# A gated cross-attention and expert kernel: projections' copies moved between ScalarE's two exponentials, values copied for four batches at once, four tiles' statistics on VectorE, routing constants behind the spread keys

## The chip, the cores and the metric

The kernel runs on one core of a Trainium2 chip. A core has five engines that work side by side, each through its own queue in order: TensorE (PE; its weight loads are shown as PEld), VectorE (DVE), ScalarE (ACT), GpSimd (POOL) and SyncE (SP, which issues DMAs here). The metric is the device time of one execution in microseconds (us); lower is better.

## What is computed

All data is fp32. There are 16 batches of 128 rows with 128 columns, and a context of 77 rows with 96 columns for each batch.

```python
x = x + tanh(g_xattn) * xattn(layernorm(x), ctx)   # 16 heads of 8 columns
x = x + tanh(g_ffn) * experts(layernorm(x))

# xattn, for each batch
q = x @ Wq.T + bq;  k, v = split(y @ Wkv.T + bkv)
att = softmax(q @ k.T / sqrt(8));  out = (att @ v) @ Wo.T + bo

# experts: four rounds over the same four experts
for r in range(4):
    w = softmax(top2(cur @ Wg[r] + bg[r]))
    cur = cur + sum_e w[e] * (gelu(cur @ W1[e] + b1[e]) @ W2[e] + b2[e])
```

## The kernel before

The kernel has two stages. The first is a loop over the 16 batches (the attention loop, "turn" b for batch b). The second is the expert stage: the rows, in two halves of 1024, are sorted by their pair of experts through DRAM, and pieces of 128 rows go through the experts, eight phases of 21 pieces. The change edits only the first stage and what stands ahead of it.

The order of the work on PE, VectorE and ScalarE is the order in which the program is written; the GpSimd instructions made through `gp` (all of the compute instructions of the loop on POOL) are pinned in program order too. So the order of every queue is written out by hand: besides the fixed body of a turn there are lists of extra work for each turn, `early`, `extra`, `amid_exp`, `amid` and `behind` (L1054 on, filled up to L1195), each called at its place.

A turn b issues in this order (L1197 to L1242):

- POOL makes the spread keys of batch b+2 (`spread_keys`, tile `km`), unless they were made before;
- PE transposes the first half of the weights of batch b (`turn_weights`, tile `ps_tr`; ScalarE copies it into `exT`), `early[b]` follows, then PE computes the scores of batch b+1 (tile `sc`, two pairs of PSUM banks), then the other transposes of batch b;
- `extra[b]`: here lie the projections of the next group of four batches;
- `weights` of batch b+1 (L874): VectorE's maximum of the first half (`mx`), difference (`d`), ScalarE's first exponential (`ex`, 128x512), VectorE's second maximum, then `put_before` (L1211), then the second difference, ScalarE's second exponential and the exponential of the rest (128x208). `put_before` issues the output projection of batch b-1 (`put_out`: `ps_o` on PE, `rows` on VectorE) and the list `amid_exp[b]`. A ScalarE instruction issued there stands between the two exponentials in ScalarE's queue;
- `attend` of batch b (tile `ps_av`), `amid[b]`, then the reciprocal and product on VectorE (`over_sums`: `rs`, `oT`), and `behind[b]`.

The projections of a group i of four batches are: `turn_ctx` (transposed context, `ps_ct`, two copies into `ctxT`), `keys` (`ps_k`, copy into `kT`), `values_left` (`ps_vr`, copy into `left`, then POOL's product `vr`), `turn_x` (`ps_xt` into `xnT`), `queries` (`ps_q` into `qT`) and `values` (`ps_v`, copied by `values_done` into `vm`, for each batch two copies of 64x64). For groups 2 and 3 they lie in turns 4 to 7 and 8 to 11: context, then keys and the rest of the values, then queries, then values. The values of group 1 lie in turn 3. All of these PSUM tiles, `ps_av`, the transposed rows `ps_c` with their copies `gT`, the logits `ps_lg` (whose matmuls are in `amid[9]` and `behind[7]`), the counts `ps_n` (`behind[10]`) and the positions `ps_pos` (`behind[11]`) come from one pool of two banks, `p_m` (L103, `bank`), handed out in turn.

Layernorm statistics are of two kinds. `Norm` computes them on VectorE (`bn_stats`, `bn_aggr`, and one small addition in `scale`); `SumNorm` on ScalarE (L285 and L287, each with a sum read out). For both, `scale` ends with a power on POOL, for SumNorm after a small POOL instruction. `norms` are those of x ahead of the attention, `norms1` those of the rows behind it; one object can hold several tiles, and its scale is computed once, with the last tile's statistics.

`routing_constants` (L319) is a generator whose steps are called one by one; two of the steps hold eight POOL instructions each on the tile `keys` (not the attention's keys).

At the end of the loop the first half's rows are stored in sorted order by eight indirect DMAs from POOL (`scatter`, L556, tile `sorted`), each made to wait for a named piece of VectorE's work, and loaded again by SP (`load`). The expert stage begins with the transposes `ps_c` of those rows into `curT`.

Of the kernel before, what the change touches and what calls it, by code (L numbers as in the profile page):

```python
# [24 lines left out]
F32 = mybir.dt.float32  # L25
I32 = mybir.dt.int32
AF = mybir.ActivationFunctionType
# [6 lines left out]
DH = 8  # L34
# [12 lines left out]
def gated_xattn_moe(  # L47
# [20 lines left out]
    nc = tc.nc  # L68
    B, L, D = x.shape
    M, C = ctx_768.shape[1:]  # L70
    R, _, E = Wg.shape
    F = W1.shape[2]
    NF = F // P
    BB = 4
    NB = B // BB
# [19 lines left out]
    gp = Pinned()  # L95
# [27 lines left out]
    bqc = const.tile([P, 1], F32, name="bqc")  # L123
# [172 lines left out]
    def tp(*args):  # L296
        nc.tensor.transpose(*args)  # L297
# [100 lines left out]
    def advance(steps, n=None):  # L398

        while n is None or n > 0:  # L400
            try:
                next(steps)
            except StopIteration:
                return
            if n is not None:
                n -= 1
# [336 lines left out]

    def norm_of(table, kind, b, n):

        norm = kind(n, f"{n}{kind.__name__[0]}")
        for j in range(n):
            table[b + j] = norm, j

# [5 lines left out]
        norm, j = norms[b]  # L755
        norm.apply(j, row(b, 0, D), x_sb[:, b, :], eng)

    def turn_ctx(i):
        ps = bank("ps_ct")
        for j in range(BB):  # L760
            tp(ps[:C, ts(j, M)], ctx_sb[:, i * BB + j, :], ident[:M, :M])
        if i == 0:
            nc.scalar.copy(ctx0[0:C, :, :].rearrange("c b m -> c (b m)"), ps[:C, : BB * M])
        else:
            spread_ctx(
                ctxT[i % 2][0:C, :, :], ps[:C, : BB * M].rearrange("c (b m) -> c b m", m=M)
            )

    def spread_ctx(dst, src):
        for lo, n, m0, m1 in ((0, 2, 0, MP), (2 * MP, HR, MP, M)):  # L770
            nc.scalar.copy(
                dst[:, :, lo : lo + n * (m1 - m0)].rearrange("c b (n m) -> c b n m", n=n),
                src[:, :, m0:m1].unsqueeze(2).to_broadcast([src.shape[0], BB, n, m1 - m0]),
            )

    def keys(i):
        ps = bank("ps_k")
        mm(
            ps[:, : BB * M].rearrange("d (b m) -> d b m", m=M), wkT,
            ctxT[i % 2][:, :, MP : MP + M] if i else ctx0, start=True, stop=True,  # L780
        )
        nc.scalar.copy(kT[:, ts(i, BB), :].rearrange("d b m -> d (b m)"), ps[:, : BB * M])

    xnTs = {}

# [6 lines left out]
        xnTs[i] = awork.tile([P, TB], F32, tag="xnT", name="xnT")  # L792
        nc.scalar.copy(xnTs[i][:, at], ps[:, at])

    def queries(i, lo=0, hi=BB):
        ps = bank("ps_q")
        at = slice(lo * P, hi * P)
        mm(ps[:, at], wqT, xnTs.pop(i)[:, at], start=True, stop=True)
        nc.scalar.activation(qT[i][:, at], ps[:, at], AF.Identity, bias=bqc)

    pss_v = {}

    def values(i, done=True):
        ps = pss_v[i] = bank("ps_v")
        for j in range(BB):
            mm(ps[:, ts(j, D)], ctxT[i % 2][:, j, 0 : 2 * MP], wvT, start=True, stop=True)
        if done:
            for j in range(BB):
                values_done(i, j, nc.scalar.copy)

    def values_done(i, j, copy):
        for k in range(2):

            copy(
                vm[i % 2][ts(k, MP), j, :]
                .rearrange("m (j n) -> m j n", j=HP)[:, :, k * DH : k * DH + D]
                .rearrange("m j (g n) -> m j g n", g=NG)[:, :, :, 0:DH],
                pss_v[i][ts(k, MP), ts(j, D)]
                .rearrange("m (g j k d) -> m k j g d", g=NG, j=HP, k=2)[:, k],
            )  # L820

    def values_left(i):

        ps = bank("ps_vr")
        for j in range(BB):
            mm(
                ps[: HR * MR, ts(j, D)], ctxT[i % 2][:, j, 2 * MP : CT], wvT,
                start=True, stop=True,
            )
        v = ps[: HR * MR, :].rearrange("m (b d) -> m b d", d=D)  # L830
        if i == 0:
            return v
        left = awork.tile([HR * MR, BB, D], F32, tag="left", name="left", bufs=1)
        nc.scalar.copy(left, v)
        values_left_done(i, left, gp)

    def values_left_done(i, v, eng):
        eng.tensor_tensor(
            vr[i % 2], v, one_r.unsqueeze(1).to_broadcast([HR * MR, BB, D]), ALU.mult
        )  # L840
# [138 lines left out]
    turn_x(0, 1, 2)  # L979
    warm_tr(2)  # L980
    queries(0, 1, 2)
    values(0, False)
    left0 = values_left(0)
    warm_tr(3)
    ex = {0: weights(scs, lambda: values_done(0, 0, nc.scalar.copy))}
    values_left_done(0, left0, nc.vector)
    for j in range(1, BB):
        values_done(0, j, nc.vector.tensor_copy)
    for j in range(2, BB):
        norms0[2].apply(j - 2, row(j, 0, D), x_sb[:, j, :], gp)  # L990
    gp.memset(ctxT[1][C : C + 1, :, :], 1.0)
# [41 lines left out]
    def stats_x1(b):  # L1033
        norm, j = norms1[b]
        norm.stats(j, row(b, D, D))
        if j == norm.n - 1:
            norm.scale()
# [4 lines left out]


    for b, kind, n in (
        (0, SumNorm, 4), (4, Norm, 3), (7, Norm, 1), (8, SumNorm, 4), (12, SumNorm, 2), (14, Norm, 2)
    ):
        norm_of(norms1, kind, b, n)
    for b, kind, n in ((4, Norm, 2), (6, SumNorm, 2), (8, Norm, 4), (12, SumNorm, 4)):
        norm_of(norms, kind, b, n)
    by_sums = [b for b in range(B) if type(norms1[b][0]) is SumNorm]  # L1050

# [23 lines left out]
    behind[1] += [lambda: norms[6][0].scale(), lambda: norm_x(6, gp), lambda: norm_x(7, gp), lambda: gp.memset(vm[1], 0.0)]  # L1075
    extra[2] += [lambda: values_left(1), lambda: turn_x(1)]
    amid[2] += [lambda: queries(1)]
    extra[3] += [lambda: values(1)]
    behind[1] += [lambda: advance(constants, 1)]
    early[2] += [lambda: advance(constants, 2)]  # L1080
    for b in (2, 5, 6):
        behind[b] += [lambda: advance(constants, 1)]
    for b, j in ((1, 8), (2, 9), (2, 10), (3, 11)):
        behind[b] += [lambda j=j: stats_x(j)]
    for b, j in ((6, 12), (7, 13), (8, 14), (8, 15)):
        amid_exp[b] += [lambda j=j: stats_x(j)]
    for i in range(2, NB):
        b = (i - 1) * BB
        at = b + i - 2
        behind[at - 1] += [  # L1090
            lambda b=b: norms[b + BB][0].scale(), lambda b=b: norm_x(b + BB, gp),
            lambda b=b: norm_x(b + BB + 1, gp),
        ]
        early[at] += [lambda b=b: norm_x(b + BB + 2, gp), lambda b=b: norm_x(b + BB + 3, gp)]
        extra[b] += [lambda i=i: turn_ctx(i)]
        extra[b + 1] += [lambda i=i: keys(i), lambda i=i: values_left(i)]
        early[b + 2] += [lambda i=i: turn_x(i)]
        extra[b + 2] += [lambda i=i: queries(i)]
        extra[b + 3] += [lambda i=i: values(i)]
    for i in range(1, NB):  # L1100
        extra[i * BB - 1] += [lambda i=i: residual(i)]
    for b in by_sums:
        if b < 13:
            amid_exp[b + 2] += [lambda b=b: stats_x1(b)]
    for b, js in ((5, (0, 1)), (6, (2, 3)), (7, (4, 5, 6))):
        behind[b] += [lambda j=j: norm_x1(j, gp) for j in js]
    behind[8] += [lambda: norm_x1(7, nc.vector)]
# [89 lines left out]
    for b in range(B):  # L1197
# [13 lines left out]
        def put_before(b=b):  # L1211
            if b:
                put_out(b - 1, o.pop(b - 1), bank_tr)
            for f in amid_exp[b]:
                f()

        if b + 1 < B:
            ex[b + 1] = weights(scs, put_before)
# [305 lines left out]
```

## Time and profile before

| | us |
|---|---|
| median of 3 runs | 441.92 (441.75 to 443.85) |
| the profiled execution, its own time | 443.99 |
| its span, first to last instruction | 442.2 |
| first expert matmuls begin in it (`ps_h`) | 107.15 |
| mean granted TensorE clock | 0.989 |

By stretches of the span, busy us of each engine:

```profile
0.00:15.00 15.00, 13.89 (x102) 12.29 (x103) 11.46 (x34) 8.11 (x20) 8.63 (x24) 1.00 0.74 200
15.00:30.00 15.00, 14.59 (x212) 10.38 (x211) 14.30 (x34) 12.94 (x37) 11.11 (x36) 1.00 0.40 133
30.00:45.00 15.00, 12.65 (x178) 9.56 (x182) 12.19 (x23) 11.67 (x36) 12.36 (x29) 1.00 0.01 2
...
90.00:105.00 15.00, 10.88 (x180) 7.57 (x180) 13.82 (x32) 10.63 (x29) 10.25 (x13) 1.00 0.24 79
```

The columns are the stretch, its length, then PE, PEld, DVE, ACT and POOL busy with the number of instructions, the granted clock, the DMA share and GB/s. In the profile's lines "L905" is a line of the program, an operation is followed by output and input tiles with partitions x elements, "x8" is a count, and the bracket at the end says how long the engine stood idle before and what ended that. Lines of a timeline begin with start and duration; a merged line covers several instructions. Where one instruction overlaps the next on its engine, the step from start to start is shorter than the duration.

### The profile page before, as it was taken

The numbers are of one execution on the slowest core, as the hardware profiler recorded it, in microseconds if no ns is written. First come the engines' busy times: TensorE is split into PE (matmuls) and PEld (weight loads), VectorE is DVE, ScalarE is ACT, GpSimd is POOL, SyncE is SP. The second block draws the span as 40 slices with busy tenths as digits, with TensorE's granted clock in tenths as the row PEclk, the third lists the DMA queues.
The fourth block names the chain that finished last, engine by engine and source line by source line (L and its number), as shares of the span: only waits on it lengthen the run. The fifth ranks groups of instructions, "written<-read, shape, count | busy, mean of one in ns | idle before, by whom it ended". The sixth has DMA issues, their size and how long they took to land.

```text
span 442.2 us, 11648 instructions
## 1 busy us (share of the span) xinstructions
PE 418.7 (95%) x4170; PEld 391.4 (88%) x4170; DVE 341.8 (77%) x888; ACT 284.4 (64%) x936; POOL 223.5 (51%) x273
## 2 busy tenths in 40 slices
PE   9998999976999989999999999999999999999991
PEld 8775767655999989999999999999999999999991
DVE  7998897897667996987798599769867985874561
ACT  4878897856566656666566656656666665666661
POOL 7488857365036515841582475259326814650061
PEclk9999999998999999999999999999999999999996
DMA  6620000013012201400130131023011301310010
GB/s 163 192 99 1 1 1 2 21 70 110 1 50 64 87 1 63 136 1 27 63 112 3 49 102 49 2 74 123 1 37 66 99 0 63 130 50 8 0 34 16
DMA packets 19709, 24.03 MB, mean 54 GB/s; under 512 B 4099, under 2 KB 16708, under 8 KB 19524
## 3 DMA queue, kind: packets, MB, share of 16 engines
q1 hardware_dynamic: 15444, 13.43, 9.7%
q0 software_dynamic: 3584, 9.70, 6.2%
q8 instruction: 33, 0.54, 0.5%
q10 hardware_dynamic: 624, 0.17, 0.2%
q14 instruction: 24, 0.20, 0.1%
HBM read 13.58 MB, written 9.71 MB: 53 GB/s over the span
## 4 chain that ended last, share of the span: by engine, by line
PE 60%; issue 11%; POOL 9%; DVE 7%; DMA 5%; ACT 4%; SPq 1%; DVEq 1%; POOLq 0%; ACTq 0%
PE ps_y L294 26%; PE ps_h L294 26%; POOL out_dram L1287 4%; DMA wall<-in_L_ffn_W_dram 2%; PE ps_c L297 2%; POOL rows L93 2%; PE ps_tr L297 1%; DVE wb L1173 1%; PE ps_av L294 1%; DMA ctx_sb<-in_ctx_dram 1%; PE sc L294 1%; DVE rows L1273 1%; DMA sorted<-rows,pos_i 1%; DMA rows<-sorted 1%; PE ps_lg L294 1%
## 5 line engine op out<-in xcount | busy, mean ns | idle before, releaser
L1259 ACT ACTIVATE hT<-ps_h,wb 128x128 f32<-128x128 f32 x512 | 145.9, 368 | 83.4 <-ACT hT L1259 50.3
L294 PE MATMUL ps_h<-curT,wb 128*128 128x128 f32 x1024 | 136.5, 277 | 0.8 <-ACT curT L413 0.7
L294 PE MATMUL ps_y<-wb,hT 128*128 128x128 f32 x1024 | 135.7, 276 | 0.0
L294 PEld LDWEIGHTS ps_h<-curT,wb 128*128 128x128 f32 x1024 | 125.7, 193 | 1.2 <-ACT curT L413 0.9
L556 POOL DMA_INDIRECT sorted<-rows,pos_i x64 | 67.6, 1056 | 114.8 <-DVE start L549 49.4
L294 PEld LDWEIGHTS ps_y<-wb,hT 128*128 128x128 f32 x1024 | 124.5, 192 | 0.0
L1173 DVE COPY wb<-wall 128x1028 f32 x128 | 109.4, 856 | 12.2 <-issue 5.6
L93 POOL TENSOR_TENSOR lp<-rows,wg_rows 128x512 f32<-128x512 f32 x48 | 72.9, 1540 | 34.1 <-DVE rows L1273 31.2
L1273 DVE SCALAR_TENSOR_TENSOR rows<-ps_y,pws,rows 128x128 f32<-128x128 f32 x126 | 43.5, 346 | 35.9 <-PE ps_y L294 35.8
L1259 ACT ACTIVATE hT<-ps_h,wall 128x128 f32<-128x128 f32 x160 | 45.5, 369 | 32.7 <-PE ps_h L294 27.9
L294 PE MATMUL ps_y<-wall,hT 128*128 128x128 f32 x320 | 43.1, 278 | 0.0
L294 PE MATMUL ps_h<-cx,wall 128*128 128x128 f32 x320 | 42.3, 275 | 0.0
L294 PEld LDWEIGHTS ps_y<-wall,hT 128*128 128x128 f32 x320 | 38.9, 192 | 2.7 <-issue 1.7
L294 PEld LDWEIGHTS ps_h<-cx,wall 128*128 128x128 f32 x320 | 38.9, 192 | 0.0
L1287 POOL DMA_INDIRECT out_dram<-res,id_i x16 | 18.9, 1181 | 35.2 <-DVE res L1278 31.2
L453 DVE TENSOR_REDUCE lg<-lp 128x4 f32<-128x512 f32 x48 | 32.3, 673 | 3.1 <-POOL lp L93 3.1
L297 PEld LDWEIGHTS ps_tr<-ident,ex 128*128 128x128 f32 (+1 forms) x160 | 16.8, 139 | 17.7 <-ACT ex L892 9.4
L297 PE MATMUL ps_tr<-ident,ex 128*128 128x128 f32 (+1 forms) x160 | 26.2, 285 | 6.0 <-ACT ex L892 4.0
L883 DVE TENSOR_REDUCE mx<-sc 128x8 f32<-128x616 f32 x32 | 25.3, 791 | 3.9 <-PE sc L294 3.8
L886 DVE TENSOR_TENSOR d<-sc,mx 128x616 f32<-128x616 f32 x32 | 25.4, 794 | 1.7
L892 ACT ACTIVATE ex<-d 128x512 f32<-128x512 f32 x32 | 20.2, 633 | 6.7 <-DVE d L886 6.5
L1273 DVE SCALAR_TENSOR_TENSOR rows<-ps_y,pwxs,rows 128x128 f32 x40 | 14.0, 350 | 12.6 <-PE ps_y L294 9.9
(230 smaller groups left out, 495.6 us busy)
## 6 DMA issues: line engine op xcount, KB each, us to landing
rows<-sorted SPq DMA_DIRECT2D x16, 528.0 KB
wall<-in_L_ffn_W_dram SPq DMA_DIRECT2D x1, 1024.0 KB
wall<-in_L_ffn_W_dram SPq DMA_DIRECT2D x4, 256.0 KB
wg_rows<-wg_turned SPq DMA_DIRECT2D x1, 1024.0 KB
sorted<-rows,pos_i POOLq DMA_INDIRECT x64
x_sb<-in_x_dram SPq DMA_DIRECT2D x3, 256.0 KB
ctx_sb<-in_ctx_dram SPq DMA_DIRECT2D x4, 115.5 KB
out_dram<-res,id_i POOLq DMA_INDIRECT x16
```

Source lines behind the costliest of these rows:

```text
L93: return lambda *a, **kw: tc.keep_in_program_order(f(*a, **kw))
L294: nc.tensor.matmul(*args, **kw)
L297: nc.tensor.transpose(*args)
L453: nc.vector.tensor_reduce(lgs[h][:, t, :], prods.pop((h, t)), AX.X, ALU.add)
L556: ins = nc.gpsimd.indirect_dma_start(out=sorted_rows[h], out_offset=bass.IndirectOffsetOnAxis(ap=pos_i[:, t : t + 1], axis=0), in_=rows[h] ...
L883: beats.append(nc.vector.tensor_reduce(mx, sv, AX.X, ALU.max))
L886: nc.vector.tensor_tensor(d[:, ts(u, HR), :].rearrange("l (g h) m -> l g h m", h=HG), sv, mx.unsqueeze(3).to_broadcast([P, 2, HG, M]), ALU ...
L892: nc.scalar.activation(ex[:, ts(u, HR * MP)].rearrange("l (h m) -> l h m", m=MP), d[:, ts(u, HR), 0:MP], AF.Exp, scale=1.0 / math.sqrt(DH),)
L1173: nc.vector.tensor_copy(wb, wall[:, ds(e, 1), :].rearrange("p o n -> p (o n)"))
L1259: nc.scalar.activation(hT[:, fc, :], ps[:, ts(fc, P)], AF.Gelu_apprx_tanh, bias=wb[:, W_B + fc : W_B + fc + 1],)
L1273: return nc.vector.scalar_tensor_tensor(at, y, w, at, ALU.mult, ALU.add)
L1287: ins = nc.gpsimd.indirect_dma_start(out=out_rows, out_offset=bass.IndirectOffsetOnAxis(ap=id_i[:, t : t + 1], axis=0), in_=res, in_offset ...
```

## The change

It has five parts.

1. `values_done` copies four batches at once: four copies of 64x128 (64 partitions, 4 batches x 4 groups x 8 columns) in place of eight of 64x64. For group 0 all four are on VectorE, where before six were on VectorE and two on ScalarE.
2. `turn_ctx`, `keys`, `queries`, `values` and `values_left` take a `put`: with it, their copies out of PSUM are not issued at once but put on the list `copies`, which `put_before` issues ahead of `amid_exp[b]`. It is used for the values of group 1, and for all projections of groups 2 and 3 but the keys of group 3 (and `turn_x`).
3. Four tiles' statistics go from ScalarE to VectorE: of the rows behind the attention tiles 1 and 3, of x tiles 14 and 15. The objects are split: tiles 0 to 3 have one each (four scales in place of one), x's 12 to 15 two.
4. The places of the statistics that stay on ScalarE change: x's tile 13 goes from turn 7 to turn 8; of the rows, tile 9 from 11 to 12 and tile 10 from 12 to 13, where tile 11 is too.
5. One step of the routing constants (the second eight instructions on `keys`) goes from `behind[2]`, ahead of the spread keys of batch 5, to `early[3]`, behind them.

The diff, its core:

```diff
-        norm = kind(n, f"{n}{kind.__name__[0]}")
+        norm = kind(n, f"{len(table)}_{b}")
...
-        nc.scalar.copy(kT[:, ts(i, BB), :].rearrange("d b m -> d (b m)"), ps[:, : BB * M])
+
+        def done():
+            nc.scalar.copy(kT[:, ts(i, BB), :].rearrange("d b m -> d (b m)"), ps[:, : BB * M])
+
+        put(done) if put else done()
...
-        if done:
-            for j in range(BB):
-                values_done(i, j, nc.scalar.copy)
...
+        if put:
+            put(lambda: values_done(i, nc.scalar.copy))
+
+    def values_done(i, copy):
+        src = pss_v.pop(i).rearrange("m (b g j k d) -> m j k b g d", b=BB, g=NG, j=HP, k=2)
+        dst = vm[i % 2].rearrange("m b (j n) -> m j b n", j=HP)
+        for j in range(HP):
+            for k in range(2):
+
+                at = ts(k, MP)
+                copy(
+                    dst[at, j, :, k * DH : k * DH + D]
+                    .rearrange("m b (g n) -> m b g n", g=NG)[:, :, :, 0:DH],
+                    src[at, j, k],
+                )
...
-        (0, SumNorm, 4), (4, Norm, 3), (7, Norm, 1), (8, SumNorm, 4), (12, SumNorm, 2), (14, Norm, 2)
+        (0, SumNorm, 1), (1, Norm, 1), (2, SumNorm, 1), (3, Norm, 1), (4, Norm, 3), (7, Norm, 1),
+        (8, SumNorm, 4), (12, SumNorm, 2), (14, Norm, 2),
...
-    for b, kind, n in ((4, Norm, 2), (6, SumNorm, 2), (8, Norm, 4), (12, SumNorm, 4)):
+    for b, kind, n in (
+        (4, Norm, 2), (6, SumNorm, 2), (8, Norm, 4), (12, SumNorm, 2), (14, Norm, 2)
+    ):
...
-    extra[3] += [lambda: values(1)]
+    copies = []
+    put = copies.append
+    extra[3] += [lambda: values(1, put)]
...
-    for b in (2, 5, 6):
+    early[3] += [lambda: advance(constants, 1)]
+    for b in (5, 6):
         behind[b] += [lambda: advance(constants, 1)]
-    for b, j in ((1, 8), (2, 9), (2, 10), (3, 11)):
+    for b, j in ((1, 8), (2, 9), (2, 10), (3, 11), (6, 14), (7, 15)):
         behind[b] += [lambda j=j: stats_x(j)]
-    for b, j in ((6, 12), (7, 13), (8, 14), (8, 15)):
+    for b, j in ((6, 12), (8, 13)):
         amid_exp[b] += [lambda j=j: stats_x(j)]
...
-        extra[b] += [lambda i=i: turn_ctx(i)]
-        extra[b + 1] += [lambda i=i: keys(i), lambda i=i: values_left(i)]
+        extra[b] += [lambda i=i: turn_ctx(i, put)]
+        extra[b + 1] += [lambda i=i: keys(i, put if i < NB - 1 else None), lambda i=i: values_left(i, put)]
         early[b + 2] += [lambda i=i: turn_x(i)]
-        extra[b + 2] += [lambda i=i: queries(i)]
-        extra[b + 3] += [lambda i=i: values(i)]
+        extra[b + 2] += [lambda i=i: queries(i, put=put)]
+        extra[b + 3] += [lambda i=i: values(i, put)]
...
-    for b in by_sums:
-        if b < 13:
-            amid_exp[b + 2] += [lambda b=b: stats_x1(b)]
+    for b, at in ((0, 2), (2, 4), (8, 10), (9, 12), (10, 13), (11, 13), (12, 14)):
+        amid_exp[at] += [lambda b=b: stats_x1(b)]
...
-            for f in amid_exp[b]:
+            for f in copies + amid_exp[b]:
                 f()
+            copies.clear()
```

## The prediction

> **What bounds the kernel now.** I read the page's shares first, then the chain that ended last (to find which part of the span the change can move), then the timelines of GpSimd (POOL), ScalarE (ACT) and TensorE (PE) over the attention loop, since the change only edits that loop.
>
> ```profile
> span 442.2 us, 11648 instructions
> PE 418.7 (95%) x4170; PEld 391.4 (88%) x4170; DVE 341.8 (77%) x888; ACT 284.4 (64%) x936; POOL 223.5 (51%) x273
> ```
>
> PE is nearly full, but most of that is the expert stage after 107 us, whose instructions the change leaves as they are. The chain shows how the loop hands over to it:
>
> ```profile
> 96.87 1.07 POOL sorted L556
> ...
> 98.24 3.70 DMA sorted<-rows,pos_i
> ...
> 102.08 3.69 DMA rows<-sorted
> ...
> 105.82 0.67 PE ps_c L297 x4
> ```
>
> The eighth store of sorted rows, its landing, the reload, then the first expert piece. So the change is worth what it does to the moment of that store (98.24). It waits for VectorE's piece of work in turns 13 and 14 of the loop, hence for the pace of the whole loop. (Turn b: first transposes of batch b, scores of b+1, the other transposes, attend of b.) The turns last 4.5 to 7.8 us; at full pace PE needs 3.7 (transposes 0.5, scores 0.74, transposes 0.71, output 0.32, attend 1.45, starts to starts) plus the turn's projections. Three things hold it back. First, GpSimd's queue:
>
> ```profile
> 34.15 2.01 POOL L93 TENSOR_SCALAR keys<-num 128x8 f32<-128x8 f32 x8
> 36.23 0.70 POOL L93 TENSOR_TENSOR km<-kT,hmask 128x308 f32<-128x308 f32 x1
> 36.89 1.27 POOL L93 TENSOR_TENSOR x_sb<-x_sb,bo_b 128x512 f32<-128x512 f32 x1
> 38.12 1.04 POOL L93 TENSOR_TENSOR rstd4N<-rstd4N,half 128x4 f32<-128x4 f32 x1
> 39.27 1.58 POOL L93 TENSOR_SCALAR rows<-x_sb,mv4N,rstd4N 128x128 f32<-128x128 f32 x2
> 40.82 0.70 POOL L93 TENSOR_TENSOR km<-kT,hmask 128x308 f32<-128x308 f32 x1
> ```
>
> POOL is without a gap from 18.2 to 43.7 us, and PE's scores wait for its spread keys (km):
>
> ```profile
> 36.98 0.80 PE L294 MATMUL sc<-km,qT 32*128 32x308 f32 x8 [1.15 <-POOL km L93]
> 41.57 0.80 PE L294 MATMUL sc<-km,qT 32*128 32x308 f32 x8
> ```
>
> The second starts 0.05 us after its km ends (41.52). Second, VectorE: maxima, differences, rows, reciprocal and product of a turn are 4.5 us of starts to starts. Third, ACT's order: where projections' copies stand ahead of the first exponential, it starts late (34.49 after copies that ended at 34.46, its difference ready at 32.68).
>
> **The change, part by part.** All by this execution's timeline (span 442.2, own time 443.99).
>
> *The first group's values* (L814): VectorE's six copies (0.232 start to start, 1.39) and ACT's two become four on VectorE with twice the elements. No 64x128 copy in runs of eight is in the trace. Bounds: twice the price of a 64x64, 0.46 each (+0.46 us in all), or fixed cost plus 64 more elements at about 1 ns, 0.30 each (-0.19). I take -0.19: it is nearest to the 128x128 copy from PSUM (0.28 long). VectorE is full from 12 to 30 us, so this moves everything behind it.
>
> *Later groups' values*: ACT's eight copies (1.73) become four; the 128x128 copy takes 0.265, so 4 x 0.275 = 1.10, saving 0.63 in turns 3, 7 and 11.
>
> *Copies between the exponentials.* With sc the start of the scores, the rows give: first exponential possible at sc+2.56 (0.84 to the maximum, 0.90, difference 0.80), second at sc+4.25. So ACT has 1.7 us between them, 0.54 of it the first exponential. Values' 1.10 fit. Context's 1.03 with statistics' 0.82 do not (second exponential 0.7 late); queries' 0.58+0.82 miss by 0.25. In turn 3 the gain is plain: first exponential at 32.5 for 34.49, transposes no longer wait 0.86.
>
> *Constants behind the spread keys; norms split in single tiles.* Ahead of km for turn 4 go 8 key steps (-2.08), but tile 0's scale comes in (0.28+0.55) and tile 1's power (0.55, as rstd1N's 0.57): km ends at 36.93-2.08+1.38 = 36.23, less 0.19: the scores at 36.1 for 36.98. For the next km nothing has left: the eight key steps are now just behind the first km, and still ahead of this one, with the bias and four norms. POOL has no gap in which to hide the 1.38, so km ends at 41.52+1.38-0.19 = 42.7 and the scores start at 42.76 for 41.57: **+1.19**. PE would be ready at 40.7. Tiles 2 and 3 add 1.38 again before the next km, which ends near 46.3; PE asks for it only near 48.8, so that costs nothing (cover: POOL's old idle 1.79 at 43.74 and PE's delay).
>
> *A copy held back holds its PSUM bank.* Projections, attend, logits, counts and positions rotate through two banks, so each matmul group waits for the copy of the group two before it. The Trainium skill (PSUM — Partial Sum Buffer, Summary: rules for kernel authors) says "Evacuate promptly", which speaks against this change altogether. The row is narrower: in turn 9
>
> ```profile
> 68.01 0.58 ACT L834 COPY left<-ps_vr 104x512 f32<-104x512 f32 x1 [0.51 <-PE ps_vr L294]
> 68.49 0.59 ACT L413 COPY gT<-ps_c 128x512 f32<-128x512 f32 x1
> 68.97 1.38 ACT L892 ACTIVATE ex<-d 128x512 f32<-128x512 f32 x2
> 70.26 0.37 ACT L896 ACTIVATE ex<-d 128x208 f32<-128x208 f32 x1
> ```
>
> ```profile
> 68.65 0.65 PE L294 MATMUL ps_av<-exT,one 128*32 128x128 f32 x16
> ```
>
> attend starts when "left" ends (68.59). By the rule all ten groups moved cost; by the row only those whose bank PE wants again before the first exponential is over. By the rule, the ten at the 0.5 to 1 us of a first exponential and a copy would be 5 to 10 us; by the row I count four places:
> - turn 5: attend needs keys' copy, which now follows the first exponential (45.3+0.54+0.38): 46.29 where PE is ready at 45.92. Shift of the next turn **+1.35**.
> - turn 7: logits wait for values' copy, as before (57.77, logits 57.83). ACT does it 0.63 faster and without waiting ahead of the exponential, but VectorE now has tile 14's statistics (0.42) behind the two constants (0.80): its idle 0.43 before the maximum at 54.34 is gone, maximum at 55.73, exponential 57.45, copies to 59.09: shift **+1.31**. The 1.7 us that ACT won go to VectorE.
> - turn 9: gT's copy stays ahead of the exponential, "left" goes behind it: ps_c ends 69.2, gT 69.27, exponential 69.75, left 70.29 to 70.87, attend 70.92 for 68.65: shift **+2.27**. This is the largest.
> - turn 10: counts need the bank of queries' copy (77.52+0.54+0.69): 78.8 for 76.15. Turn 11: positions need values' copy (82.99+0.54+1.10): 84.7 for 81.67. Shift **+3.0** for PE, +2.65 for VectorE's maximum in turn 12.
>
> *Statistics.* Four tiles leave ACT (4 x 0.82) and cost VectorE 0.42 to 0.60 each. Tile 1 (turn 2) lies in the 0.55 that VectorE waited at 30.97, tile 3 (turn 4) in its wait for the late scores of turn 5, tile 15 (turn 7) just fits, tile 14 is counted. Two tiles now stand in turn 13 (10 and 11): 1.64 between the exponentials. Tile 11's sums end 98.6 by the shifted clock; POOL's scale of 8 to 11 and the seventh and eighth store are queued behind them: **+0.3**.
>
> *Sum at the eighth store*: +3.0 + 0.3 = +3.3. VectorE has a wait of 1.23 us in turn 13 (88.84, for PE) that no row explains; without it in both kernels the same walk gives +2.9, VectorE's maximum in turn 14 being then due 2.6 later and the store 0.3 more. I take **+3.1**. The profiled execution took 443.99, 2.07 above the median of 441.92 (443.85 also occurred); the difference is put on the median: 441.92 + 3.1 = **445.0 us**.
>
> **The rivals.**
> 1. *The freed exponential decides; faster.* PE's waits for the exponential are 4.0 us in four places; 0.86 (35.18) and 0.73 (65.36) are of the kind the change removes, and the wait for km of 1.15 goes too: -2.7, so 439.2. For it: these are the waits that the trace names. It needs POOL to give back the 1.38 before km of turn 5 (if that km ended by 40.7) and attend of turn 9 not to be held. Against it: POOL's gapless row, and the bank order. Chance 0.13.
> 2. *Only POOL's part lasts.* +1.2, the bank waits covered by slack elsewhere (PE loses 1.16 in turn 13 and 1.47 in turn 14 waiting for others): 443.1. Within what a measurement can tell from no change, which I set at 0.5% (2.2 us). Chance 0.20.
> 3. *More than counted*: the four-batch copies cost twice a 64x64, so nothing is saved (+0.65 at VectorE's start, +0.6 in turns 7 and 11), or turn 13's unexplained wait grows: 447. Chance 0.11. This is also the case in which "four at once" does not do what it says.
> The likeliest keeps 0.56, from 443.6 to 446.6.
>
> **How the numbers follow.** Slower by over 0.5% (above 444.1): nearly all of the likeliest (0.54) and case 3: 0.65. Within: case 2 and an edge: 0.22. Faster: 0.13. The range from 442.0 to 447.5 leaves out rival 1 and the far end of case 3.
>
> **What would show it.** Right: in the profile after, POOL gapless up to km of turn 5, which ends near 42.7, and the scores of that turn waiting for it about 2 us; attend of turn 9 starting as "left" ends, near 71; the first exponential of turn 3 near 32.5; the eighth store 3 us later; the expert stage's length unchanged. Wrong: the scores of turn 5 before 42, POOL with gaps before, or attend of turn 9 starting as the transposes' copies allow.

## The result and the profile after

| | before | after |
|---|---|---|
| median of 20 runs each, us | 442.16 (440.04 to 445.46) | 445.87 (441.85 to 448.3) |
| the profiled execution, its own time, us | 443.99 | 445.78 |
| its span, us | 442.2 | 444.0 |
| first expert matmuls (`ps_h`) begin, us | 107.15 | 109.25 |
| from there to the end of the span, us | 335.05 | 334.75 |

The ratio of after to before is 1.0061, 95% interval 1.0039 to 1.0084: about 2.7 us slower (0.0061 x 442), inside the predicted range. It is not the quotient of the medians (1.0084): the runs lie in groups, and a median can jump from one group to the next. In the two profiles all of the difference arises in the attention loop. Two things are easily misread here. The two profiled executions differ by only 1.8 us, less than the medians (3.7), because the profile of before has 1.9 us in turn 13 that after's has not (7.04 us from scores to scores, where the same turn takes 5.11 and 5.12 in experiments 10 and 11). And the profile of after runs 0.36 us late from the start (VectorE's first values' copies begin at 12.76 for 12.40).

The page of after begins with the same picture as before: PE full, ScalarE's 30 instructions fewer and VectorE's nine more.

```profile
span 444.0 us, 11631 instructions
PE 418.9 (94%) x4170; PEld 392.4 (88%) x4170; DVE 343.4 (77%) x897; ACT 278.8 (63%) x906; POOL 229.3 (52%) x278
```

Next comes what PE waited for in the loop, 29 to 100 us. Each row names the matmul and its line, the releaser, the microseconds in all, how often, and the longest. First before:

```profile
PE ps_tr L297 <- ACT ex L892: 3.1, 3, 1.5
PE ps_tr L297 <- ACT exT L905: 1.4, 2, 1.2
PE sc L294 <- POOL km L93: 1.1, 1, 1.1
PE ps_c L297 <- POOL rows L93: 0.4, 1, 0.4
...
```

The same view of after:

```profile
PE sc L294 <- POOL km L93: 3.6, 2, 2.2
PE ps_tr L297 <- ACT ex L906: 1.8, 3, 1.1
PE ps_o L294 <- ACT exT L919: 1.2, 5, 0.5
PE ps_lg L294 <- ACT vm L826: 0.7, 1, 0.7
PE ps_pos L294 <- ACT vm L826: 0.6, 1, 0.6
PE ps_av L294 <- ACT gT L413: 0.5, 1, 0.5
PE ps_n L294 <- ACT qT L806: 0.4, 1, 0.4
...
```

The change did what it says on ScalarE: the waits for the exponential fall from 3.1 to 1.8 us. The waits for the spread keys rise from 1.1 to 3.6, and four waits for copies out of the two banks, which the list of before doesn't have, appear: three for copies that the change holds back (0.7, 0.6 and 0.4) and one for `gT` (0.5), whose bank attend takes in turn 9. GpSimd's timeline of after shows where the first comes from:

```profile
34.37 0.19 POOL L93 TENSOR_SCALAR rstd<-mv 128x1 f32<-128x1 f32 x1
34.65 1.10 POOL L93 TENSOR_TENSOR rstd<-rstd,half 128x1 f32<-128x1 f32 x2
35.72 0.70 POOL L93 TENSOR_TENSOR km<-kT,hmask 128x308 f32<-128x308 f32 x1
36.50 2.01 POOL L93 TENSOR_SCALAR keys<-num 128x8 f32<-128x8 f32 x8
38.57 1.28 POOL L93 TENSOR_TENSOR x_sb<-x_sb,bo_b 128x512 f32<-128x512 f32 x1
39.81 1.03 POOL L93 TENSOR_TENSOR rstd<-rstd,half 128x4 f32<-128x4 f32 x1
40.95 1.59 POOL L93 TENSOR_SCALAR rows<-x_sb,mv,rstd 128x128 f32<-128x128 f32 x2
42.50 0.70 POOL L93 TENSOR_TENSOR km<-kT,hmask 128x308 f32<-128x308 f32 x1
```

The eight key steps now stand behind the first `km` (35.72) and ahead of the second (42.50); two scales (1.35 us, 34.37 to 35.72) have come in ahead of the first. No row has an idle bracket. PE's timeline shows who pays, in turns 4 and 5 and then in turn 9:

```profile
36.47 0.80 PE L294 MATMUL sc<-km,qT 32*128 32x308 f32 x8 [1.41 <-POOL km L93]
...
43.26 0.91 PE L294 MATMUL sc<-km,qT 32*128 32x308 f32 x8 [2.19 <-POOL km L93]
44.10 1.54 PE L297 MATMUL ps_tr<-ident,ex 128*128 128x128 f32 x6
...
48.03 0.64 PE L294 MATMUL ps_av<-exT,one 128*32 128x128 f32 x16
...
71.30 0.64 PE L294 MATMUL ps_av<-exT,one 128*32 128x128 f32 x16 [0.45 <-ACT gT L413]
```

The scores of turn 5 wait 2.19 us and start at 43.26 for 41.57. The row to be surprised at is the next: six transposes take 1.54 us, where six take 0.87 and 0.88 at this place in experiments 6 and 9. By stretches of 3.41 us, with the granted clock in the third column from the end:

```profile
40.45:43.86 3.41, 1.22 (x16) 0.69 (x12) 1.92 (x6) 2.29 (x8) 3.30 (x5) 0.99 0.02 5
43.86:47.27 3.41, 3.41 (x16) 2.78 (x13) 2.30 (x3) 1.81 (x4) 2.83 (x6) 0.50 0.00 0
47.27:50.68 3.41, 3.41 (x68) 2.92 (x70) 2.40 (x6) 1.96 (x5) 1.99 (x17) 1.00 0.00 0
```

In the stretch that holds the wait PE was busy for 1.22 us of 3.41; in the next the granted clock is 0.50, then 1.00 again. In the profile of before the only such stretch is at 107.6, behind the wait for the reload of the sorted rows.

The end of the loop, from the chain of after in order of time: the reload and the first expert pieces, 2.1 us later than before. The eighth store starts on POOL at 100.33 for 98.24.

```profile
104.06 3.82 DMA rows<-sorted
...
107.92 0.67 PE ps_c L297 x4
```

### The profile page after: what moved, and what is told of

Read it like the earlier page. It is cut to its first block, busy times and chain, and to the rows that moved or that the text cites. A ratio compares the mean times of both kernels' runs of the same rounds, so it can differ in the third digit from the quotient of the medians.

```text
span 444.0 us, 11631 instructions
## 1 busy us (share of the span) xinstructions
PE 418.9 (94%) x4170; PEld 392.4 (88%) x4170; DVE 343.4 (77%) x897; ACT 278.8 (63%) x906; POOL 229.3 (52%) x278
## 4 chain that ended last, share of the span: by engine, by line
PE 63%; DVE 11%; issue 11%; POOL 9%; ACT 3%; DMA 1%; DVEq 0%; POOLq 0%
PE ps_y L294 26%; PE ps_h L294 26%; POOL out_dram L1308 4%; DVE d L900 3%; DVE mx L897 2%; PE ps_c L297 2%; POOL rows L93 1%; PE ps_tr L297 1%; PE ps_warm L294 1%; PE sc L294 1%; DVE wb L1193 1%; PE ps_bh L294 1%; DMA rows<-sorted 1%; ACT ex L906 1%; PE ps_lg L294 1%
## 5 line engine op out<-in xcount | busy, mean ns | idle before, releaser
L556 POOL DMA_INDIRECT sorted<-rows,pos_i x64 | 71.4, 1116 | 108.4 <-DVE start L549 57.6
L919 ACT COPY exT<-ps_tr 128x512 f32<-128x512 f32 x32 | 18.5, 578 | 11.8 <-PE ps_tr L297 11.5
```

The source lines that it names most:

```text
L556: ins = nc.gpsimd.indirect_dma_start(out=sorted_rows[h], out_offset=bass.IndirectOffsetOnAxis(ap=pos_i[:, t : t + 1], axis=0), in_=rows[h] ...
```

## The experiments

Theory A, from the prediction with one addition: GpSimd's order puts 1.4 us ahead of the spread keys of turn 5, the wait lets the clock fall to half, and that is most of the loss. Theory B: the copies held behind the exponential keep their banks, and that is most of it. Theory C: it is VectorE's additional statistics. Each batch of four kernels shared its runs of the kernel before. In the first batch (experiments 1 to 4) these had a median of 443.91, against 442.16 to 442.89 elsewhere, so ratios are best compared within a batch. The kernel after did not run in the first batch: the ratios of 1 to 3 can't be put against its 1.0061, and what they show is read from their traces.

**1. Scales of the rows' tiles 0 to 3 later.** After, with these four scales in turn 5.

```diff
-        if j == norm.n - 1:
+        if j == norm.n - 1 and b > 3:
             norm.scale()
...
+    early[5] += [lambda k=k: norms1[k][0].scale() for k in range(4)]
```

> The changed kernel with the four scales of the rows' tiles 0 to 3 issued in turn 5, behind the spread keys that PE waits for, so that nothing of the split norms stands ahead of them on GpSimd. GpSimd theory: the spread keys for turn 5 end 1.4 us earlier (41.8 on the changed kernel's clock), PE waits 0.8 us for them in place of 2.19, TensorE's clock stays full behind that wait, and the expert stage begins 2 to 2.6 us earlier; time about 443.5. Bank theory (copies held back cost most): turn 5 starts earlier but at most 1 us of it lasts; time 445.

Measured: 444.59, ratio 0.9998 (0.9968 to 1.0027). Scores of turn 4 start at 35.10, those of turn 5 at 41.89, still behind a wait of 2.20, because PE came there earlier. Attend follows them by 3.56 us: no half clock there, although the wait is as long as in after. PE was busy for more of the stretch of 3.41 us in which it waited, 1.81 us in place of 1.22:

```profile
40.29:43.70 3.41, 1.81 (x16) 1.32 (x17) 2.08 (x6) 2.02 (x6) 3.41 (x6) 1.00 0.00 0
```

The norms' 1.35 us are a real part of the lateness: set to zero at turn 3, as in the table below, the scores of turn 12 come 1.40 later than in before, where they come 2.85 later in after. Taken away alone, they leave the wait.

**2. The second eight constants later as well.** Experiment 1 plus:

```diff
-    early[3] += [lambda: advance(constants, 1)]
+    early[5] += [lambda: advance(constants, 1)]
```

> The same, and the second eight routing constants are issued in turn 5 too. GpSimd theory: the spread keys of turns 4 and 5 no longer hold PE at all, scores of turn 5 start near 41 in place of 43.26, no low clock behind them, the expert stage begins about 3.3 us earlier than in the changed kernel; time 442.4, that of the kernel before or a little less. Bank theory: not over 1 us better than the changed kernel, 445.

Measured: 444.73, ratio 1.0014 (0.999 to 1.0038). The scores of turn 5 start at 40.43 with a wait of 0.40, but in turn 7 the transposes of the first norm rows wait for GpSimd:

```profile
52.95 0.33 PE L297 MATMUL ps_c<-ident,rows 128*128 128x128 f32 x1 [1.02 <-POOL rows L93]
53.72 0.33 PE L297 MATMUL ps_c<-ident,rows 128*128 128x128 f32 x1 [0.45 <-POOL rows L93]
```

The clock is at half behind that, from 55.0 to 58.4. So it is not the place of one step that binds. GpSimd has too much to do before turn 7; moved inside that stretch, work only moves the wait (the shift at turn 12 is 1.57).

**3. Three kinds of copies at once again.** After, with keys, left rows and queries copied where before copied them (context and values still held).

```diff
-        extra[b + 1] += [lambda i=i: keys(i, put if i < NB - 1 else None), lambda i=i: values_left(i, put)]
+        extra[b + 1] += [lambda i=i: keys(i), lambda i=i: values_left(i)]
-        extra[b + 2] += [lambda i=i: queries(i, put=put)]
+        extra[b + 2] += [lambda i=i: queries(i)]
```

> The changed kernel with the copies of keys, of the rest of the values and of queries issued at once again; those of context and values stay between the exponentials. GpSimd theory: scores of turn 5 unchanged at 43.2, PE's waits in turns 9 and 10 (0.45 and 0.41) go, time 445.2. Bank theory: 1.5 us or more come back, time 444 or less.

Measured: 444.98, ratio 1.000 (0.9971 to 1.0029). The waits of turns 9 and 10 (0.45 and 0.41) are gone, that of turn 11 is 0.85 for 0.60; the 2.21 us of turn 5 and the half clock behind it (44.9 to 48.3) stay. This ratio taken alone favours B, but after was not in the batch. The trace doesn't favour it: set to zero at turn 3, the scores of turn 12 come 2.75 later than in before, against 2.85 in after, so only 0.1 us of the loop's lateness goes with the three kinds of held copies. Experiment 12 repeats the question on another base.

**4. Constants alone.** Before, with the second eight constants behind the spread keys of turn 4, as the change has them.

```diff
-    for b in (2, 5, 6):
+    early[3] += [lambda: advance(constants, 1)]
+    for b in (5, 6):
         behind[b] += [lambda: advance(constants, 1)]
```

> The kernel before with one part of the change alone: the second eight routing constants behind the spread keys of batch 5. GpSimd theory: the wait of 1.15 us for the spread keys in turn 4 goes, but the spread keys for turn 5 stand behind the same work as before, scores of turn 5 start at 41.57 still, and the time stays at that of the kernel before (0.3 us either way). Rival, that the named wait is the price: 1.1 us faster.

Measured: 443.88, ratio 0.9989 (0.9968 to 1.0009). PE's timeline:

```profile
36.10 0.80 PE L294 MATMUL sc<-km,qT 32*128 32x308 f32 x8
41.95 0.80 PE L294 MATMUL sc<-km,qT 32*128 32x308 f32 x8 [1.12 <-POOL km L93]
```

The wait of 1.15 in turn 4 has become one of 1.12 in turn 5, and nothing is won.

**5. The kernel after once more**, in the second batch (experiments 5 to 8).

> The changed kernel itself, as the measure for the others on the same chip. Every theory: 1.006 of the kernel before, about 2.7 us more. Clock theory: its time falls into steps of about 1.8 us, as the half-clock stretches behind PE's waits are one or two.

Measured: 444.8, ratio 1.0054 (1.0013 to 1.0095). The wait in turn 5 is 2.22, the half clock runs from 43.6 to 47.0, attend follows the scores by 4.78. So this is no accident of one execution.

**6. PE kept busy in the wait, too long.** After, with matmuls of zeros ahead of the scores of turns 4 and 5.

```diff
+        if b in (4, 5):
+            warm_tr({4: 10, 5: 18}[b])
         if b + 1 < B:
             scs = scores(b + 1, kms.pop(b + 1))
```

> The changed kernel with 10 and 18 idle matmuls on zeros ahead of the scores of turns 4 and 5, where PE waits for the spread keys; nothing else. Clock theory: the scores of turn 5 still start when the spread keys end (about 43.2), but the granted clock stays at 1.00 behind them in place of 0.50 for 3.4 us, attend of that turn starts 3.5 us behind the scores in place of 4.8, and the time falls by 1.2 us. Queue theory alone (the clock costs nothing of its own): attend follows the scores as late as before, time the same.

Measured: 445.21, ratio 1.0059 (1.0037 to 1.0082). A miss of my own: each matmul of zeros appears as two in the profile, and the 36 of turn 5 took 4.18 us and ended 2.4 us behind the keys (scores at 45.68). Attend followed by 3.56, but the lateness ate that. Experiment 9 repeats it with the right count.

**7. Single scales alone.** Before, with the norm of tiles 0 to 3 split in four (statistics left on ScalarE).

```diff
-        (0, SumNorm, 4), (4, Norm, 3), (7, Norm, 1), (8, SumNorm, 4), (12, SumNorm, 2), (14, Norm, 2)
+        (0, SumNorm, 1), (1, SumNorm, 1), (2, SumNorm, 1), (3, SumNorm, 1), (4, Norm, 3), (7, Norm, 1), (8, SumNorm, 4), (12, SumNorm, 2), (14, Norm, 2)
```

> The kernel before with one part alone: the rows' tiles 0 to 3 get a scale each, all on ScalarE's sums as before. It adds 0.83 us on GpSimd for each tile, two of them ahead of the spread keys for turn 5, and removes the common scale of 1.23 later. GpSimd theory: scores of turn 5 start 1.7 us later than in the kernel before (43.2), PE waits some 1.6 us for them; time 1 to 2.5 us more, the most with a half-clock stretch behind the wait. Bank theory: no loss over 0.5 us, as no copy is moved.

Measured: 443.43, ratio 1.0026 (1.0009 to 1.0044). Scores of turn 4 at 37.77 behind a wait of 2.07, the clock at half from 39.2 to 42.6, scores of turn 5 at 43.57 for 41.57. The wait stands one turn earlier, since the constants are still in front; the price is of the kind that A names. The shift at turn 12 is 1.43.

**8. Scales and constants out of the way.** After, with the four scales in turn 5 (experiment 1) and the constants behind the norm rows that turn 7 needs.

```diff
-    early[3] += [lambda: advance(constants, 1)]
-    for b in (5, 6):
-        behind[b] += [lambda: advance(constants, 1)]
+    early[7] += [lambda: advance(constants, 2)]
+    amid[9] += [lambda: advance(constants, 1)]
```

> The changed kernel with GpSimd's queue put in order: the four scales in turn 5, the last two GpSimd steps of the routing constants in turn 7 where GpSimd waits over 4 us, their VectorE step in turn 9 where VectorE waits 1.9 us for logits. GpSimd theory: no wait of PE for spread keys or rows in turns 4, 5 and 7, 3 us less than the changed kernel, so at the kernel before or up to 1 us under it. Bank theory: 1 us less than the changed kernel.

Measured: 442.26, ratio 0.9984 (0.996 to 1.0009); the runs lie between 438.49 and 443.7, and the profile is of one of the three fastest (438.6). Scores of turn 5 at 39.31, first expert matmuls at 102.97. With GpSimd relieved, the loss of the change is gone, and a gain over before is not shown.

**9. PE kept busy in the wait, the right length.** As 6, with `{4: 6, 5: 7}`.

> The kernel after with 12 matmuls of zeros ahead of the scores of turn 4 and 14 ahead of those of turn 5, sized from the run with 20 and 36 (0.116 us each), so that they end when the spread keys do (36.3 and 43.2) and not 2.4 us behind. Clock theory: TensorE is not idle in the 2.2 us wait, the granted clock stays 1.00 from 43 to 48, the output's matmuls (attend) follow the scores of turn 5 by 3.5 us and not 4.8, later turns are 1.2 us earlier, ratio to the kernel before 1.003. Rival: a 3.4 us stretch at half clock is only moved to the next place with waits (the run with too many zeros had one at 64 us), and the ratio stays at 1.005 to 1.006.

Measured: 445.24, ratio 1.006 (1.004 to 1.0079). PE's timeline in turn 5:

```profile
40.59 1.73 PE L294 MATMUL ps_warm<-zero 128*128 128x128 f32 x14
42.95 0.80 PE L294 MATMUL sc<-km,qT 32*128 32x308 f32 x8 [0.64 <-POOL km L93]
43.69 0.88 PE L297 MATMUL ps_tr<-ident,ex 128*128 128x128 f32 x6
...
46.52 0.64 PE L294 MATMUL ps_av<-exT,one 128*32 128x128 f32 x16 [0.34 <-ACT kT L785]
```

The stretches of the same kernel:

```profile
39.75:43.16 3.41, 2.77 (x38) 2.39 (x34) 2.32 (x6) 2.67 (x9) 3.30 (x5) 1.00 0.02 5
43.16:46.58 3.42, 3.08 (x30) 2.31 (x30) 2.60 (x5) 1.91 (x5) 3.23 (x6) 1.00 0.00 0
```

The scores can start no earlier than in after (42.95, with 0.31 of it the earlier start of this execution), but PE is busy 2.77 us of the stretch in place of 1.22: the next one is at full clock, the six transposes take 0.88 for 1.54, attend follows the scores by 3.57 for 4.77. The half clock is therefore a consequence of PE's idleness, and costs 1.20 us here. The loop in this execution is earlier by that still in turn 14 (scores at 94.81 for 96.35, 0.34 of it from its earlier start). The median isn't: in this profile another half stretch has come up in the expert stage, at 162 to 165.4, behind a wait of 1.61 for VectorE that before and after have too, without the clock falling there. So the theory's expectation held for the place, and the rival's for the time. Only one execution of each kernel has a trace, but the mean granted clock of every run is on record: over the 20 runs of this kernel it averages 0.988, over the 20 of after 0.983. There was less half clock on the whole (the mean takes in the idle end of the kernel too), and the ratio is the same. So the 1.20 us are shown for this place in the trace; that they are a part of the loss in the time is not shown.

**10. GpSimd's part alone.** Before, with experiments 4 and 7 together: constants behind the keys of turn 4 and four single scales; copies, statistics and banks as before.

> The kernel before with GpSimd's part of the change alone: second constants behind the spread keys of turn 4, four single scales for tiles 0 to 3; copies, statistics and banks as before. If GpSimd's order makes the first half of the loss: scores of turn 5 start near 42.7 for 41.57 after a wait of about 2 us, the waits of turns 9 to 11 for copies are absent, and the ratio is 1.003 (1.1 us) to 1.005 (with a stretch at half clock behind the wait). If the held copies make all of the loss: 1.000. If GpSimd makes all of it: 1.006.

Measured: 445.25, ratio 1.0063 (1.004 to 1.0085), as much as the whole loss. (All four tiles stay on ScalarE's sums here, so 0.28 us more than in the change stand ahead of the keys of turn 5.) PE's timeline, then the stretches:

```profile
36.55 0.80 PE L294 MATMUL sc<-km,qT 32*128 32x308 f32 x8
...
44.23 0.96 PE L294 MATMUL sc<-km,qT 32*128 32x308 f32 x8 [2.93 <-POOL km L93]
```

```profile
41.32:44.74 3.42, 0.52 (x8) 0.31 (x8) 0.62 (x2) 1.35 (x4) 3.31 (x5) 1.00 0.02 5
44.74:48.15 3.41, 3.41 (x20) 2.63 (x13) 2.31 (x3) 1.28 (x3) 2.38 (x5) 0.50 0.00 0
```

All of the wait stands in turn 5: in turn 4 the keys are in time, since PE comes there later (its transposes wait 0.86 for the exponential, as before). The half clock follows. The two parts don't add up: alone they shift turn 12 by -0.13 (experiment 4) and +1.43 (experiment 7), together by +2.82, since only together do they stand ahead of the same keys. Of the four outcomes expected, "GpSimd makes all of it: 1.006" came in.

**11. Before, with only its constants moved**, as in 8: two steps to turn 7, one to turn 9.

```diff
-    for b in (2, 5, 6):
-        behind[b] += [lambda: advance(constants, 1)]
+    early[7] += [lambda: advance(constants, 2)]
+    amid[9] += [lambda: advance(constants, 1)]
```

> The kernel before with only its constants moved: GpSimd's two steps from turns 2 and 5 to the front of turn 7, VectorE's step from turn 6 to turn 9. If GpSimd's load ahead of the spread keys is what holds the first turns: scores of turn 4 near 35.8 (36.98 before), of turn 5 near 40.4 (41.57 before), and the ratio is 0.995 to 0.998. If the gain of the kernel after with the same move comes from the change's copies instead, this one stays at 1.000.

Measured: 440.36, ratio 0.9943 (0.9922 to 0.9963): faster than before and after. What PE waits for in its loop, 29 to 100 us:

```profile
PE ps_tr L297 <- ACT ex L892: 3.1, 4, 1.0
PE ps_o L294 <- ACT exT L905: 0.6, 3, 0.2
PE ps_tr L297 <- ACT exT L905: 0.5, 2, 0.2
...
```

No wait for `km` and none for `rows` is left. The waits for the exponential, which the change set out to remove, are all still there, and it is the fastest kernel of the study.

**12. Experiment 8 with keys, left rows and queries copied at once** (the diff of 3 on top).

> The kernel after with scales and constants moved (0.9984), and keys, left rows and queries copied at once again, as in the kernel before. If the held banks cost: the waits for the copies of gT (0.45) in turn 9 and of queries (0.41) in turn 10 are gone, the loop is 0.5 to 1 us shorter, ratio 0.996. If the exponentials of those turns become late by the same amount, or the waits are slack: 0.998 as without it.

Measured: 441.5, ratio 0.9968 (0.9949 to 0.9987). The waits for gT and queries are gone, the one in turn 11 is 0.85 again; set to zero at turn 3, the scores of turns 10 and 12 start 0.6 and 0.4 us earlier than in 8 (68.94 and 80.51 for 69.54 and 80.87). The step in the ratio is of that size (0.0016, 0.7 us), but the intervals overlap: holding these three kinds of copies costs a few tenths of a microsecond or nothing, and no gain from it is seen. Against 11 (same batch) this kernel is 1.1 us behind in the median, so the rest of the change doesn't pay either where GpSimd is relieved; in the traces 0.65 of it stand in turn 13, which takes 5.77 us with two tiles' sums between the exponentials and 5.12 in 11.

**The loop, turn by turn.** Start of the scores against before, in us, each kernel set to zero at the scores of turn 3:

| turn | before, start | after | GpSimd's part alone (10) | constants moved (11) |
|---|---|---|---|---|
| 4 | 36.98 | -0.67 | -1.21 | -1.22 |
| 5 | 41.57 | +1.53 | +1.88 | -1.14 |
| 6 | 47.41 | +2.94 | +3.29 | -1.03 |
| 7 | 53.51 | +1.93 | +2.80 | -2.03 |
| 8 | 59.30 | +2.54 | +2.82 | -2.02 |
| 10 | 72.08 | +2.48 | +2.81 | -1.96 |
| 12 | 83.04 | +2.85 | +2.82 | -1.95 |
| 13 | 87.63 | +2.78 | +2.82 | -1.95 |
| 14 | 94.67 | +1.52 | +0.89 | -3.87 |

GpSimd's part alone makes its shift in turns 5 and 6, gives 0.5 of it back in turn 7 and then keeps the rest. The kernel after makes much the same shift in turns 5 and 6, wins 1.0 by turn 7 (0.4 of it the wait of the row transposes for GpSimd's rows, which before has and after has not) and gives 0.9 back by turn 12. In turn 14 all columns drop by 1.3 to 1.9: that is the 1.9 us of turn 13 in the profile of before, of which after has used up 0.67.

## Why the prediction came out right, step by step

The number held, and so did the first step of the sum, GpSimd's queue. The rest of the sum came out by balance, which is luck: of the 3.1 us only 1.19 were put on GpSimd's order, the others on held copies, VectorE and statistics, and experiment 10, which has none of these, is as late in turn 12 (+2.82) as after (+2.85).

- **The four-batch copies: right.** Predicted were 1.20 us for four on VectorE and 1.10 on ScalarE; they took 1.19 (from 12.76) and 1.06 (from 33.41). The first exponential of turn 3 was due near 32.5 and starts at 32.86, 0.36 of it the late start of that execution. So ScalarE has its gain there; the scores of turns 4 and 5 then wait for the spread keys all the same (1.41 and 2.19 us).
- **Spread keys of turn 5 (+1.19 predicted): right.** The keys were to end near 42.7 and ended at 43.20, of which 0.36 is the late start of that execution; POOL gapless, the scores waiting about 2 us (2.19). Experiment 10 shows that GpSimd's order alone is enough for the whole loss, and experiment 8 that the loss goes when GpSimd is relieved.
- **Keys' copy ahead of attend in turn 5 (+1.35 for the next turn): the size was off.** The next scores came 2.94 late, not 1.35. The hold itself was right: the wait of attend for the keys' copy, put at 0.37 (46.29 less 45.92), shows as 0.34 in experiments 1 and 9, where no half clock covers it. The missing term is the half clock behind the wait, 1.20 us in the traces of after and experiment 9. I had priced a wait at its length only.
- **Turn 7, VectorE bound (+1.31): right in kind.** The maximum waits for nothing and starts at 57.16; statistics and constants stand gapless ahead of it, as walked, later by the term just named.
- **Turn 9, "attend starts as left ends" (+2.27): wrong.** This is the step that failed. Attend started at 71.30, before the copy of left began:

```profile
70.66 0.58 ACT L413 COPY gT<-ps_c 128x512 f32<-128x512 f32 x1 [0.90 <-PE ps_c L297]
71.14 0.64 ACT L906 ACTIVATE ex<-d 128x512 f32<-128x512 f32 x1
71.68 0.58 ACT L846 COPY left<-ps_vr 104x512 f32<-104x512 f32 x1
```

  It waited 0.45 for gT. In before the transposed rows' copy ran until 69.08 and attend started at 68.65, as left ended: there it took left's bank. I carried that over. But before issued left's copy ahead of gT's, and after issues gT's first; in both, attend took the bank whose copy is issued first. Experiments 3 and 12 try it: with the rest of their kernels (after and that of 8) kept, they issue left's copy ahead of gT's again, and attend starts as left's ends, while gT's still runs. In 12, ScalarE's rows and PE's:

```profile
65.41 0.58 ACT L846 COPY left<-ps_vr 104x512 f32<-104x512 f32 x1 [0.51 <-PE ps_vr L294]
65.89 0.59 ACT L413 COPY gT<-ps_c 128x512 f32<-128x512 f32 x1
```

```profile
66.05 0.65 PE L294 MATMUL ps_av<-exT,one 128*32 128x128 f32 x16
```

  So the bank pool of this program doesn't go by the order in which the groups came, as I had it ("the group two before it"), but here by which copy comes first. Between turns 8 and 10 the shift did not grow (2.54 and 2.48), where I had put almost 1.0.
- **Turns 10 and 11 (to +3.0): right in kind.** The waits named are there, for queries' copy (0.41) and values' copy (0.60). The growth was put at 0.73 and is 0.37 (2.48 to 2.85 at turn 12); the level comes near +3.0 only because the half clock's 1.20 stands in for what turn 9 and these turns lack.
- **Turn 13 (+0.3): too small.** With two tiles' sums between the exponentials the turn takes 5.78 us, against 5.11 and 5.12 in experiments 10 and 11: 0.67. The eighth store, due 3 us later, came 2.1 later in the profiles; without the 1.9 us that before has in this turn it would be some 4 (an estimate).
- **The unexplained 1.23 us of turn 13** are VectorE's wait ahead of its reciprocal. The profiles of before and of experiment 4 have it (1.23 and 1.25), those of experiments 1 to 3 have 1.70 at the same place; in these five the turn takes 7.0 to 7.6 us from scores to scores, in the other nine 5.1 to 5.8. All four kernels of the first batch have it and none of the eight later ones. It comes and goes between kernels that have the same turn 13 (before and 11, after and 3), so it isn't in the order of the work; what it is stays open. It is why the profiles differ by less than the medians.
- **The Trainium skill's rule "Evacuate promptly"** (PSUM — Partial Sum Buffer, Summary: rules for kernel authors) was weighed as five to ten microseconds if it held for all ten moved groups. The profile shows waits for three held copies (0.7, 0.6, 0.4) and one for gT (0.5), 2.2 us in all, and the fall of the exponentials' waits (1.3) pays for part; with three kinds of them copied at once again, the shift at turn 12 fell by 0.1 us (3 against after) and 0.4 (12 against 8). So the narrow reading was the nearer one, and these runs give the held copies no price clear of noise.
- **The rivals.** "The freed exponential decides" needed GpSimd to have the time; experiment 11 shows that the reserve lay there: it gains 0.57% with all the waits for the exponential in place. "Only POOL's part lasts" had the mechanism nearer than the likeliest case and the price too low (1.2 us for 0.0063 x 442 = 2.8); in the trace of experiment 10 the half clock follows its wait too. Theories B and C aren't needed: experiment 10 has no held copies, none of the additional statistics, and as large a loss. Of theory A the first half, GpSimd's order, is shown by experiments 8, 10 and 11; the half clock's share in the time isn't (experiment 9).

## What to carry to other kernels

A chain of "PE waits for X" rows tells where time is lost, not whose work to move: before moving work within one engine's queue, sum all that this engine must finish by each deadline, because inside a gapless stretch every step moved only moves the wait (experiments 2 and 4), while work with no deadline moved out of it wins at once (11). Price a wait of PE in a trace at its length plus a possible half clock behind it: waits of 2.2 us were followed by one in after and not in experiment 1. And where a change alters the order of two copies that free banks, work out anew which of them frees the next group's bank: in turn 9 here it was the one issued first, in both orders.

## What the hardware showed unasked

- **The granted clock falls to 0.50 for stretches of 3.41 us on a fixed grid.** Two stretches of one execution start a whole number of such lengths apart: 43.86 and 108.71 in after (19.0 x 3.413), 39.22 and 107.49 in experiment 7 (20.0), 44.74 and 109.59 in experiment 10 (19.0). With such a grid laid through the first half-clock stretch of each of the fourteen profiles, from 29 to 113 us, every window in which PE was busy for 46% of the time or less is followed by one at half clock (15 of 15); at 52 to 80% 6 of 64 are, and above 80% none of 230, leaving out windows that are at half clock themselves. The Trainium skill (TensorE: Matmul & The Clock Gate, What's actually happening) describes a free-running window of 3413 ns that halves the clock when idle; these profiles agree with its length. They differ on "idle": in after a wait of 2.19 us, shorter than the window, was enough, with PE busy for 1.22 of the 3.41 us of the window.
- **The runs of one kernel spread over 5.4 us (before) and 6.5 us (after)**, for after in groups near 442.0, 443.7, 445.8, 446.7 and 447.9. One half stretch takes up to 1.7 us (an estimate, half of 3.41), and the profiles hold from one to four of them ahead of the kernel's end. But the groups aren't simply numbers of stretches: the mean granted clock of after's runs is 0.989 near 442.0, 0.985 to 0.986 near 443.7, 0.978 to 0.979 near 445.8 (but 0.988 in the profiled run), 0.981 near 446.7 and 0.982 near 447.9, so the fastest group has the most full clock and the slowest not the least. What else makes the groups isn't shown.
